# Another order of ScalarE's and VectorE's work in the first eleven steps of a fused recurrent mixer

## The chip, the cores and the metric

The kernel runs on one core of a Trainium2 chip. The metric is the device time of one execution in microseconds (us). TensorE is called PE in the profile (PEld is its weight load), VectorE is DVE, ScalarE is ACT, GpSimd is POOL and SyncE is SP.

## What is computed

```python
xn = layernorm(x)                                  # x: 4 x 256 x 512
zxbcdt = xn @ in_proj_w.T                          # gate 8192, x 8192, B and C 8*128 each, dt 128
xBC = silu(conv4(xBC) + conv_b)                    # causal, 4 taps, per channel
dt = softplus(dt + dt_bias); A = -exp(A_log)       # 128 heads of 64 channels, 8 groups
# per head: a linear recurrence; it is taken here in 2 chunks of 128 positions per sequence
Y[i] = sum over j <= i of (C_i . B_j) * exp(sum of A*dt over j+1..i) * x_j * dt_j
y = (Y + D*x) * silu(gate)
y = y * rsqrt(mean of y*y over a group of 1024 channels + eps) * norm_w
s = y @ out_proj_w.T
g = silu(ffn(xn))                                  # ternary weights, 512 -> 1792 -> 512
out = x + s * g
```

## The kernel before

All arithmetic is float32. A first part, `front`, makes the layer norm, the feed-forward network, dt, the scores C.B of the 8 groups and the running decay sums of the first 20 heads; in the profiled execution its last products on PE end at about 313.5 us. What follows is a loop over 64 channel tiles of 128 channels (two heads each), `for i in range(CT)`. Its order is written out by hand: under a manual schedule each engine works through its instructions in the order of the program, and waits are only for data and for buffers. The loop is a pipeline in which three tiles are under way at once. Step i

- projects tile i: x by way of `px` and `pq`, the gate by way of `pz` and others. It is a seven-product scheme of the Strassen kind. In the order of PE: **A** px = a11*x11, **B** pq = s1*t1, **C** px += s2*t2, **D** the first half of pz += a12*x21, **E** px += s3*t3, **F** the second half of pz, **G** px += a22*t4, **H** pq += s4*x22. A to H all have line 173. What stands in px is taken out by ACT after A (to pz, line 832), after C (to the gate's second half gT, line 842, "the gate's copy"), after E (to xpad, line 874) and after G (to xpad, line 902). Since C, E and G add to the same bank px, each has to wait for the copy before it;
- finishes tile i-1: convolution's SiLU (line 186), the exponentials of its two decay matrices m (line 627), "meet" (lines 630 and 631: m and the off-diagonal block mo are multiplied by the group's scores gm, on DVE), transposes of x on PE (tp, line 637, two ahead of E and two ahead of G, four behind H), values v on DVE (lines 645, 654), and 24 products for y (py, line 681);
- gates tile i-2 on DVE (line 688) and squares it on ACT (line 863); an accumulating DMA on POOL's queue (line 934) adds the squares to sqacc.

Steps 0 to 9 (`fill`) do no output projection yet. In these the sums of squares are made right behind the exponentials. In steps 1 to 10 (`lead`) both exponentials of tile i-1 stand in step i; from step 11 on the first of them is made at the end of the step before. Where ACT goes from SiLU to Exp or back, the trace shows an ACT_TABLE_LOAD of 1.28 us. On DVE the order behind "meet" is line 894 (xpad += pq, for which H waits, since it adds to pq), the values, the sums of the next weights (lines 142 to 146), the taps of the convolution (line 181) and line 915 (gT += pq). In steps 3 to 6 ACT scales two tiles of the output weights (line 882), in steps 7 and 8 DVE makes one sum of 1.22 us each for the output projection (lines 726, 727), and in step 10 the first sums of the output projection (lines 717 to 720), the sum of squares of group 0 (`norm_sums`, PE line 699, ACT line 702) and two scans (line 189) come in. Weights, rows of decays and scores come through SP's queue.

Of the kernel before, what the change touches and what calls it, by code (L numbers as in the profile page):

```python
# [51 lines left out]
NB = 4  # L52
L = 256
NC = 2
T = NB * L
# [21 lines left out]
HALF = T // 2  # L77
# [4 lines left out]
def mixer_ffn(ctx: ExitStack, tc: tile.TileContext, x, in_w, conv_w, conv_b, dt_bias, a_log, d_col,  # L82
              norm_w, out_w, gate_t, up_t, down_t, gate_s, up_s, down_s, out):
    nc = tc.nc
# [34 lines left out]
    gm = mc.tile([P, ROW], F32, name="gm")  # L119
# [16 lines left out]
    def blocks(w):  # L136
        return [w[:, n, k:k + 2, :] for n in (0, 1) for k in (0, 2)]

    def combine_to(s1, s2, s4, s3, w):

        a11, a12, a21, a22 = blocks(w)
        nc.vector.tensor_add(s1, a21, a22)
        nc.vector.tensor_sub(s2, s1, a11)
        yield
        nc.vector.tensor_sub(s4, a12, s2)
        nc.vector.tensor_sub(s3, a11, a21)
        yield

    def factors(w, s):
        a11, a12, a21, a22 = blocks(w)  # L150
        return a11, a12, a22, s[:, 0], s[:, 1], s[:, 2], a21
# [15 lines left out]
    def by_batch(v):  # L167
        return v.rearrange("p (b l) -> p b l", l=L)

    def product(pp, a, b, start, ks=range(KT // 2)):  # L170

        for k in ks:
            nc.tensor.matmul(pp, a[:, k, :], b[:, k, :], start=start and k == 0,  # L173
                             stop=k == KT // 2 - 1, skip_group_check=not start)

    def last_tap(i, xT, xpad):
        nc.scalar.mul(xT, xpad[:, :, TAPS - 1:], cw[:, i, TAPS - 1:TAPS])  # L177

    def conv_taps(i, xT, xpad, taps=range(TAPS - 1)):
        for k in taps:  # L180
            nc.vector.scalar_tensor_tensor(xT, xpad[:, :, k:k + L], cw[:, i, k:k + 1], xT,  # L181
                                           ALU.mult, ALU.add)

    def conv_silu(i, xT):
        xf = xT.rearrange("p b l -> p (b l)")
        nc.scalar.activation(xf, xf, AF.Silu, bias=cb[:, i:i + 1])  # L186

    def decay_scan(m):
        nc.vector.tensor_tensor_scan(m, m, after, 0.0, ALU.add, ALU.mult)  # L189
# [419 lines left out]
    def load_rows(ct):  # L609
        ms = []  # L610
        for h in range(2):
            m = mp.tile([P, T], F32, name="m")
            n = 2 * ct + h
            nc.sync.dma_start(m, early[n] if ct < EARLY else rows[n, 0:T].partition_broadcast(P))
            ms.append(m)
        return ms

    def load_off(ct):
        offs = []
        for h in range(2):  # L620
            m = mop.tile([P, NB * P], F32, name="mo")
            nc.sync.dma_start(m, rows[2 * ct + h, T:].partition_broadcast(P))
            offs.append(m)
        return offs

    def decay_exp(m):
        nc.scalar.activation(m, m, AF.Exp)  # L627

    def meet(m, off):
        nc.vector.tensor_mul(m, m, gm[:, 0:T])  # L630
        nc.vector.tensor_mul(off, off, gm[:, T:])

    def transposed(xT, c, bs=range(NB), tp=None):
        if tp is None:
            tp = ps_t.tile([P, NB, P], F32, name="tp", tag="t")
        for b in bs:
            nc.tensor.transpose(tp[:, b, :], xT[:, b, c * P:(c + 1) * P], ident)  # L637
        return tp
# [12 lines left out]
    def values_1(ct, xT):  # L651
        tp = transposed(xT, 1)
        v = xsp.tile([P, NB, 2, HD], F32, name="v")
        nc.vector.tensor_tensor(
            v, tp.rearrange("p b (h d) -> p b h d", d=HD),
            dt[:, 1, :, 2 * ct:2 * ct + 2].unsqueeze(3).to_broadcast([P, NB, 2, HD]), ALU.mult)
        return v

    def y_begin(ct, xT):

        ps = []
        for i in range(2):
            py = ps_y.tile([P, 2, L], F32, name="py", tag="y")
            nc.scalar.mul(py, xT[:, 2 * i:2 * i + 2, :], dcol[:, ct:ct + 1])
            ps.append(py)
        return ps
# [110 lines left out]
    with tc.manual_schedule():  # L777
        nc.sync.dma_start(gm, scores[0])
        ms, offs = {0: load_rows(0)}, {0: load_off(0)}
        xTs, gTs, yps, wos, rights, toms = {}, {}, {}, {}, {}, {}  # L780
        sqacc = sq = rs = ya = outs = left = nxt = ob = sa = sb = sc = None
        for i in range(CT):
            r, g = i % PER_G, i // PER_G
            here, old, older = True, i >= 1, i >= 2
# [8 lines left out]
            def project_out(between):  # L793
                nonlocal sa, sb, sc, outs
                if on % 2 == 0:
                    sa = osp.tile([P, NC, HID], F32, name="sa")
                    sb = osp.tile([P, NC, HH], F32, name="sb")
                    sc = osp.tile([P, HH], F32, name="sc", bufs=2)
                    outs = out_first(left, rights[og], leave)
                for n in range(4 - on % 2):  # L800
                    next(outs)
                    if n == 1:
                        between()
# [10 lines left out]
            fill = og < 0  # L814
# [11 lines left out]
            if here:  # L826
                a11, a12, a22, s1, s2, s4, s3 = a
                px, pq, pz = [ps_proj.tile([P, HALF], F32, name=f"p{n}", tag="proj")
                              for n in "xqz"]
                gT = gtp.tile([P, T], F32, name="gT")  # L830
                product(px, a11, x11, True)
                nc.scalar.copy(pz, px)
            lead = old and i - 1 < LEAD
            if lead:
                conv_silu(i - 1, xTs[i - 1])
                decay_exp(ms[i - 1][0])
            elif old:
                decay_exp(ms[i - 1][1])
            if here:
                product(pq, s1, t1, True)  # L840
                product(px, s2, t2, False)
                nc.scalar.copy(gT[:, HALF:], px)  # L842
                if lead:
                    decay_exp(ms[i - 1][1])
                if i >= EARLY:
                    decay_scan(ms[i][0])

                product(pz, a12, x21, False, (0,))
            if old:
                tp0 = transposed(xTs[i - 1], 0, (0, 1))  # L850
                meet(ms[i - 1][0], offs[i - 1][0])
                meet(ms[i - 1][1], offs[i - 1][1])
                if r == 0 and here:
                    nc.sync.dma_start(gm, scores[g])
                if not fill:
                    yps[i - 1] = y_begin(i - 1, xTs[i - 1])

            def square():
                nonlocal sq, sqacc
                yf = yg.rearrange("p b l -> p (b l)")  # L860
                first = (i - 2) % PER_G == 0
                sq = sqp.tile([P, T], F32, name="sqacc" if first else "sq")
                nc.scalar.activation(sq, yf, AF.Square)  # L863
                if first:
                    sqacc = sq

            if older and fill:
                square()
            if here:
                product(px, s3, t3, False)  # L870
                product(pz, a12, x21, False, (1,))
                if old:
                    transposed(xTs[i - 1], 0, (2, 3), tp0)
                nc.scalar.copy(xpad_h[1], by_batch(px))
            if old and fill:
                yps[i - 1] = y_begin(i - 1, xTs[i - 1])
# [27 lines left out]
            if fill:  # L904
                s = scp.tile([P, 3, KT // 2, P], F32, name="s")
                sums = combine_to(s[:, 0], s[:, 1], s[:, 2], blocks(w)[2], w)
                a = factors(w, s)
                next(sums)
                xTs[i] = xtp.tile([P, NB, L], F32, name="xT")
                last_tap(i, xTs[i], xpad)  # L910
                conv_taps(i, xTs[i], xpad, (0,))
                if old:
                    vs.append(values_1(i - 1, xTs[i - 1]))
            if here:
                nc.vector.tensor_add(gT[:, HALF:], gT[:, HALF:], pq)  # L915
                if og >= 0 and on == 0:
                    rs = small.tile([P, NT], F32, name="rs2", bufs=2)
                    nc.vector.reciprocal(rs, sd)
# [5 lines left out]
            if here:  # L924
                nc.scalar.activation(gT[:, 0:HALF], pz, AF.Silu)
                if og >= 0:
                    project_out(lambda: nc.scalar.activation(gT[:, HALF:], gT[:, HALF:], AF.Silu))
                else:
                    nc.scalar.activation(gT[:, HALF:], gT[:, HALF:], AF.Silu)
            if old:  # L930
                y_products(yps[i - 1], vs, ms.pop(i - 1), offs.pop(i - 1), fill)
            if older and (i - 2) % PER_G:
# [41 lines left out]
        last, ob = CT - 1, NB - 1  # L974
# [3 lines left out]
        decay_exp(ms[last][1])  # L978
        py = y_begin(last, xTs[last])
        vs = values_0(last, transposed(xTs[last], 0))  # L980
        for m, off in zip(ms[last], offs[last]):
            meet(m, off)
        sa = wp.tile([P, NC, KT, P], F32, name="w").rearrange("p n k m -> p n (k m)")
        sb = scp.tile([P, 3, KT // 2, P], F32, name="s")[:, 0:2].rearrange("p n k m -> p n (k m)")
        sc = osp.tile([P, HH], F32, name="sc", bufs=2)
# [14 lines left out]
        yg, gT = ygp.tile([P, NB, L], F32, name="yg"), gTs.pop(last)  # L1000
# [105 lines left out]
```

## Time and profile before

| | |
|---|---|
| median of three runs | 1743.87 us (1742.74 to 1744.98) |
| profiled execution, its own time | 1743.98 us |
| its span, from the first to the last instruction | 1742.3 us |
| granted clock of PE | 0.999 |
| PE busy, DVE busy, ACT busy | 1718.9, 1446.9, 1068.7 us |
| steps 0 to 10 | 313.5 to 500.1 us of the span |
| step 0, step 1 (from A to the next A) | 12.2, 18.7 us |
| steps 2 to 9 | 16.24, 16.32, 16.33, 16.32, 16.32, 16.58, 16.28, 16.24 us |
| step 10 | 25.0 us |

The profiled execution's time is 1.7 us above its span. In a timeline, each row has the start in us, the duration in us, the engine, the line, the operation, what it writes and reads, the number of instructions merged, and in brackets the idle time of the engine just before with what ended it. The matmuls' durations overlap, so the distance from one row's start to the next is what counts on PE.

### The profile page before, as it was taken

What the parts mean: (1) busy time and instruction counts of PE and PEld (TensorE: products, weight loads), DVE (VectorE), ACT (ScalarE), POOL (GpSimd) and SP (SyncE); (2) the same over time, 40 slices, a digit from 0 to 9 for tenths busy, and PEclk for the clock granted to TensorE, in tenths of its full rate; (3) what the DMA queues carried; (4) which work ended last, traced back from release to release, by engine and by line L of the source; (5) the groups of instructions that cost most, each with busy time, mean ns of one, the idle gap of its engine ahead of it and who ended that gap; (6) DMA issues with size and microseconds to landing.
All of it is one profiled execution on the core that took longest, in us unless ns stands there. A gap on an engine that the chain in (4) does not pass through costs nothing.

```text
span 1742.3 us, 22580 instructions
## 1 busy us (share of the span) xinstructions
PE 1718.9 (99%) x8494; PEld 1108.2 (64%) x8494; DVE 1446.9 (83%) x1742; ACT 1068.7 (61%) x1418; POOL 211.7 (12%) x238
## 2 busy tenths in 40 slices
PE   9999999999999999999999999999999999999999
PEld 7566666555566666666666666666666666666687
DVE  5768878577898898889888988898888888888876
ACT  4544333588776666666666666666666676667740
POOL 3312323000000000111011101110111011101110
PEclk9999999999999999999999999999999999999999
DMA  6266565567746676777677667776766677757785
GB/s 226 71 205 225 211 206 207 174 209 228 215 161 206 200 214 190 208 203 214 190 208 202 202 189 217 200 200 185 210 200 198 182 211 200 215 163 212 212 234 167
DMA packets 161931, 347.27 MB, mean 199 GB/s; under 512 B 15136, under 2 KB 52896, under 8 KB 161824
## 3 DMA queue, kind: packets, MB, share of 16 engines
q1 hardware_dynamic: 139136, 292.89, 48.8%
q0 software_dynamic: 22688, 52.96, 17.1%
q8 instruction: 67, 1.10, 0.2%
q14 instruction: 40, 0.33, 0.1%
HBM read 236.48 MB, written 81.00 MB: 182 GB/s over the span
## 4 chain that ended last, share of the span: by engine, by line
PE 89%; DVE 3%; ACT 3%; DMA 3%; issue 1%; SPq 1%; POOL 0%; ACTq 0%; DVEq 0%
PE px L173 26%; PE po L737 22%; PE pq L173 13%; PE py L681 10%; PE pz L173 7%; PE tp L637 3%; PE pp L288 3%; DMA w<-in_in_w 2%; PE pf L296 2%; PE pg L463 1%; PE pv L699 1%; DVE bT L181 1%; ACT m L627 1%; ACT xT L186 1%; DVE cT L181 0%
## 5 line engine op out<-in xcount | busy, mean ns | idle before, releaser
L173 PE MATMUL px<-xc,w 128*128 128x512 f32 x576 | 273.2, 597 | 8.4 <-ACT xpad L427 5.7
L181 DVE SCALAR_TENSOR_TENSOR xT<-xpad,cw,xT 128x1024 f32<-128x1024 f32 x192 | 246.1, 1282 | 14.2 <-ACT xT L177 10.0
L189 DVE TENSOR_TENSOR_SCAN m<-m,after 128x1024 f32<-128x1024 f32 x108 | 246.5, 2282 | 0.0
L737 PE MATMUL po<-wo,ya 128*128 128x256 f32 x768 | 176.5, 379 | 0.0
L630 DVE TENSOR_TENSOR m<-m,gm 128x1024 f32<-128x1024 f32 x128 | 155.0, 1211 | 21.1 <-ACT m L627 21.0
L681 PE MATMUL py<-m,v 128*64 128x128 f32 x2048 | 160.3, 276 | 0.0
L934 POOL DMA_DIRECT2D sqacc<-sq x54 | 46.1, 854 | 884.2 <-ACT sq L863 811.8
L173 PEld LDWEIGHTS px<-xc,w 128*128 128x128 f32 x576 | 98.9, 190 | 84.1 <-issue 68.9
L737 PEld LDWEIGHTS po<-wo,ya 128*128 128x128 f32 x768 | 141.5, 190 | 17.0 <-issue 0.2
L173 PE MATMUL pz<-xnT,w 128*128 128x512 f32 x288 | 145.8, 592 | 0.0
L173 PE MATMUL px<-xnT,w 128*128 128x512 f32 x288 | 141.8, 615 | 0.0
L173 PE MATMUL px<-xc,s 128*128 128x512 f32 x288 | 135.8, 594 | 2.3 <-ACT cpad L427 1.8
L173 PE MATMUL pq<-xnT,s 128*128 128x512 f32 x288 | 136.2, 595 | 0.1
L173 PE MATMUL pq<-xc,s 128*128 128x512 f32 x288 | 135.4, 592 | 0.7 <-DVE gT L915 0.7
L627 ACT ACTIVATE m<-m 128x1024 f32<-128x1024 f32 x128 | 135.4, 1058 | 0.7
L637 PEld LDWEIGHTS tp<-ident,xT 128*128 128x128 f32 x512 | 67.7, 140 | 100.0 <-issue 87.3
L681 PEld LDWEIGHTS py<-m,v 128*64 128x64 f32 x2048 | 117.1, 137 | 20.2 <-issue 19.1
L737 PE MATMUL po<-tw,sy 128*128 128x256 f32 x512 | 115.9, 379 | 0.0
L737 PEld LDWEIGHTS po<-tw,sy 128*128 128x128 f32 x512 | 97.2, 190 | 13.2
L842 ACT COPY gT<-px 128x512 f32<-128x512 f32 x64 | 37.3, 583 | 103.0 <-PE px L173 103.0
L681 PE MATMUL py<-mo,v 128*64 128x128 f32 x1024 | 99.4, 273 | 0.0
L173 PEld LDWEIGHTS pq<-xc,s 128*128 128x128 f32 x288 | 54.6, 190 | 69.9 <-issue 61.2
(178 smaller groups left out, 3118.3 us busy)
## 6 DMA issues: line engine op xcount, KB each, us to landing
m<-rows SPq DMA_DIRECT2D x108, 512.0 KB, 6.5
w<-in_in_w SPq DMA_DIRECT2D x144, 256.0 KB, 6.9
mo<-rows SPq DMA_DIRECT2D x128, 256.0 KB, 7.2
gated<-yg SPq DMA_DIRECT2D x64, 512.0 KB, 8.2
ya<-gated SPq DMA_DIRECT2D x30, 1024.0 KB, 7.1
sqacc<-sq POOLq DMA_DIRECT2D x54, 512.0 KB, 5.9
wo<-in_out_w SPq DMA_DIRECT2D x64, 256.0 KB, 7.0
acc<-sa POOLq DMA_DIRECT2D x23, 512.0 KB, 5.9
```

The lines of the kernel that those rows point to most:

```text
L173: nc.tensor.matmul(pp, a[:, k, :], b[:, k, :], start=start and k == 0, stop=k == KT // 2 - 1, skip_group_check=not start)
L181: nc.vector.scalar_tensor_tensor(xT, xpad[:, :, k:k + L], cw[:, i, k:k + 1], xT, ALU.mult, ALU.add)
L189: nc.vector.tensor_tensor_scan(m, m, after, 0.0, ALU.add, ALU.mult)
L288: nc.tensor.matmul(pp, w[:, k * P:(k + 1) * P], part[:, k, :], start=(k == 0 and part is xh), stop=(k == KT - 1 and part is xl))
L296: nc.tensor.matmul(pf, part[:, i * P:(i + 1) * P], wd, start=(f == 0 and part is hh), stop=(f == FT - 1 and part is hl))
L627: nc.scalar.activation(m, m, AF.Exp)
L630: nc.vector.tensor_mul(m, m, gm[:, 0:T])
L637: nc.tensor.transpose(tp[:, b, :], xT[:, b, c * P:(c + 1) * P], ident)
L681: nc.tensor.matmul(py[d, q * P:(q + 1) * P], v[:, b, h, :], m, start=False, stop=True, skip_group_check=True)
L737: nc.tensor.matmul(po, a[:, k, :], b[:, k, :], start=start and k == 0, stop=k == HG - 1, skip_group_check=not start)
L842: nc.scalar.copy(gT[:, HALF:], px)
L934: nc.gpsimd.dma_start(sqacc, sq, accum_op=ALU.add)
```

## The change

In steps 1 to 10 the gate's copy (line 842) stands ahead of both exponentials in ACT's order instead of between them. In step 1 the SiLU of tile 0 also goes behind the gate's copy, and its four transposes of the first chunk all go behind F. "Meet" multiplies both off-diagonal blocks first and both m after that, in every step. In steps 2 to 9 the square goes from behind the exponentials to the end of the step, behind the gate's SiLU. In step 0, line 915 goes ahead of the first tap on DVE. Nothing is added or left out.

```diff
-    def meet(m, off):
-        nc.vector.tensor_mul(m, m, gm[:, 0:T])
-        nc.vector.tensor_mul(off, off, gm[:, T:])
+    def meet(ms, offs):
+        for off in offs:
+            nc.vector.tensor_mul(off, off, gm[:, T:])
+        for m in ms:
+            nc.vector.tensor_mul(m, m, gm[:, 0:T])
...
             lead = old and i - 1 < LEAD
-            if lead:
+            if lead and i > 1:
                 conv_silu(i - 1, xTs[i - 1])
-                decay_exp(ms[i - 1][0])
-            elif old:
+            elif old and not lead:
                 decay_exp(ms[i - 1][1])
             if here:
                 product(pq, s1, t1, True)
                 product(px, s2, t2, False)
                 nc.scalar.copy(gT[:, HALF:], px)
+                if i == 1:
+                    conv_silu(0, xTs[0])
                 if lead:
+                    decay_exp(ms[i - 1][0])
                     decay_exp(ms[i - 1][1])
                 if i >= EARLY:
                     decay_scan(ms[i][0])
 
                 product(pz, a12, x21, False, (0,))
             if old:
-                tp0 = transposed(xTs[i - 1], 0, (0, 1))
-                meet(ms[i - 1][0], offs[i - 1][0])
-                meet(ms[i - 1][1], offs[i - 1][1])
+                tp0 = transposed(xTs[i - 1], 0, (0, 1) if i > 1 else ())
+                meet(ms[i - 1], offs[i - 1])
...
-            if older and fill:
-                square()
             if here:
                 product(px, s3, t3, False)
                 product(pz, a12, x21, False, (1,))
                 if old:
-                    transposed(xTs[i - 1], 0, (2, 3), tp0)
+                    transposed(xTs[i - 1], 0, (2, 3) if i > 1 else range(NB), tp0)
                 nc.scalar.copy(xpad_h[1], by_batch(px))
...
                 last_tap(i, xTs[i], xpad)
+                if i == 0:
+                    nc.vector.tensor_add(gT[:, HALF:], gT[:, HALF:], pq)
                 conv_taps(i, xTs[i], xpad, (0,))
...
             if here:
-                nc.vector.tensor_add(gT[:, HALF:], gT[:, HALF:], pq)
+                if i:
+                    nc.vector.tensor_add(gT[:, HALF:], gT[:, HALF:], pq)
...
                     nc.scalar.activation(gT[:, HALF:], gT[:, HALF:], AF.Silu)
+            if older and fill:
+                square()
             if old:
                 y_products(yps[i - 1], vs, ms.pop(i - 1), offs.pop(i - 1), fill)
...
-        for m, off in zip(ms[last], offs[last]):
-            meet(m, off)
+        meet(ms[last], offs[last])
```

## The prediction

> **What bounds the kernel.** I read the shares of engines and the chain that ended last first, both on the page.
>
> ```profile
> PE 1718.9 (99%) x8494; PEld 1108.2 (64%) x8494; DVE 1446.9 (83%) x1742; ACT 1068.7 (61%) x1418; POOL 211.7 (12%) x238
> ...
> PE 89%; DVE 3%; ACT 3%; DMA 3%; issue 1%; SPq 1%; POOL 0%; ACTq 0%; DVEq 0%
> ```
>
> PE is busy for 99% of the span and holds 89% of the chain. So an edit on ACT or DVE counts only by the time that PE waits, and nothing later gives a delay back. Next I read PE's timeline in step 2.
>
> ```profile
> 349.71 1.02 PE L173 MATMUL pz<-xnT,w 128*128 128x512 f32 x2
> 350.57 0.38 PE L637 MATMUL tp<-ident,xT 128*128 128x128 f32 x2
> 351.06 1.98 PE L173 MATMUL px<-xc,w 128*128 128x512 f32 x4
> 352.89 1.02 PE L173 MATMUL pz<-xnT,w 128*128 128x512 f32 x2
> 353.74 0.38 PE L637 MATMUL tp<-ident,xT 128*128 128x128 f32 x2
> 353.96 1.88 PE L173 MATMUL px<-xc,w 128*128 128x512 f32 x4
> 355.68 1.88 PE L173 MATMUL pq<-xnT,s 128*128 128x512 f32 x4
> ```
>
> These are D, two transposes, E, F, two transposes, G, H. From start to start the second pair of transposes takes 0.22 us, the first 0.49: E waits 0.27. G takes 1.72, E 1.83: a product after a wait costs 0.11 more (as B and E of step 1 do). So 0.38 us a step can be had at E, no more. ACT's timeline shows why, and what stands next to it.
>
> ```profile
> 347.02 1.15 ACT L186 ACTIVATE xT<-xT,cb 128x1024 f32<-128x1024 f32 x1
> 348.19 1.28 ACT L627 ACT_TABLE_LOAD   x1
> 349.48 1.06 ACT L627 ACTIVATE m<-m 128x1024 f32<-128x1024 f32 x1
> 350.44 0.57 ACT L842 COPY gT<-px 128x512 f32<-128x512 f32 x1
> 350.91 1.06 ACT L627 ACTIVATE m<-m 128x1024 f32<-128x1024 f32 x1
> 351.87 1.05 ACT L863 ACTIVATE sqacc<-yg 128x1024 f32<-128x1024 f32 x1
> 353.09 0.59 ACT L874 COPY xpad<-px 128x512 f32<-128x512 f32 x1 [0.17 <-PE px L173]
> ```
>
> The gate's copy ends at 351.01, and E starts 0.05 later. But the table load and the first exponential run while PE still makes C; they end about when C does. The copy for G ends at 353.68, 0.28 before G.
>
> **The change, part by part: steps 2 to 9.** I keep step 2's clock. C gives way to D at 349.71. A copy can start 0.20 after that (the xpad copy at 353.09 starts 0.20 after F took E's place), so the gate's copy runs from 349.91 to 350.50. E can start at 350.79: the 0.38 goes. Now the question is where the table load stands. The trace shows it in front of the activation that needs it and behind a copy that itself waits:
>
> ```profile
> 94.59 0.59 ACT L366 COPY dt<-tp 128x512 f32<-128x512 f32 x1 [5.12 <-PE tp L365]
> 95.19 1.28 ACT L558 ACT_TABLE_LOAD   x1
> 96.49 0.69 ACT L558 ACTIVATE sg<-pp,gs 128x512 f32<-128x512 f32 x1
> ```
>
> There ACT stood idle for 5.12 us and the load still came after the copy, 0.60 after its start, and the function 1.30 after that. So after the change the load no longer runs beside C: 349.91 copy, 350.50 load, 351.80 first exponential, 0.96 to the second (350.91 to 351.87 is such a distance) at 352.76, 0.96 to the xpad copy at 353.72, 0.59 for it, 0.05 to PE: G at 354.36. PE would be ready at 350.79 + 1.72 + 0.85 + 0.22 = 353.58. So G waits 0.78 and pays 0.11 for it. Net per step: -0.38 + 0.78 + 0.11 = **+0.51**. The square's 0.95, gone from this place, is already in that chain; without it the loss would be 1.46. Eight steps: +4.1.
>
> [...]
>
> What hides the rest. The square at the step's end: ACT's next copy waits for A (1.95 us idle before 362.77, the copy behind A), and the square needs 0.95 of it. Nothing stands behind the square on ACT but that copy; without this cover it would delay C by up to 0.95. DVE: both mo (0.60 each) move into DVE's wait of 2.26 us before m, so only two m follow: first m at 352.89, second 1.14 later at 354.03, line 894 at 355.17 to 355.86. It was at 354.05, so it is 1.1 late, but H starts at 354.36 + 1.83 = 356.19; 0.33 is left. The taps wait for ACT, as before, 2.0 us behind H.
>
> Where that cover is thinner:
> - Steps 3 to 6 (line 882): the copy behind G started 0.35 after H (step 3: 372.27 against 371.92), now 353.72 + 0.48 + 1.24 + 1.22 = 356.66, 0.47 after H. The values for the last y products were already just in time, so +0.11 each, **+0.4**.
> - Step 7: DVE's sum of line 726 (1.14) stands ahead of line 894. Line 894 ended at 437.39 and H started at 437.45; now the second m starts 4.32 after D, as in step 2, at 435.56, line 726 at 436.70, line 894 runs from 437.83 to 438.51, H at 438.56: +1.11, that is **+0.6** above the 0.51.
> - Step 8: line 727 stands ahead of the weights' sums and the taps. Line 894 comes 5.46 after D, at 453.29, the taps 0.60 + 0.60 + 0.60 + 1.13 + 0.46 + 0.34 behind it at 457.02; that is 2.7 after H (454.31) instead of 2.1, and the values for the last y products come 0.6 late: **+0.6**.
> - Step 10: ACT makes copy, load, exponentials, two products for y (1.23) and the xpad copy: G at 486.2, as before (486.30). But DVE: first m at 483.52 (was 481.20), second 484.66, four sums of 0.67 (lines 717 to 720), line 894 from 488.46 to 489.14; H at 489.2 instead of 488.10: **+1.1**.
>
> **Steps 0 and 1.** On PE B of step 1 waits 0.69 for line 915, and E 1.76 for the gate's copy:
>
> ```profile
> 328.28 1.98 PE L173 MATMUL pq<-xc,s 128*128 128x512 f32 x4 [0.69 <-DVE gT L915]
> ...
> 334.82 1.98 PE L173 MATMUL px<-xc,w 128*128 128x512 f32 x4 [1.76 <-ACT gT L842]
> ```
>
> Line 915 needs H of step 0, done when A starts at 325.72; 0.2 later it runs, until 326.60. Then B follows A at 327.44, C 329.16, D 330.88, E 331.74 (the gate's copy at 331.08 to 331.65). The tap now waits 0.17 longer, but no longer has line 915 behind it: the taps end at 330.22, before the copy. Then ACT: SiLU 331.55, load 332.72, exponentials 334.01 and 334.97, xpad copy 335.93 to 336.52, G 336.57 (was 337.72). PE would be ready at 334.84, so it waits here. A of step 2 moves from 344.46 to 343.4: **-1.0**.
>
> **Steps 11 to 63 and the tail.** Only the order of "meet" changes there. The list of waits has DVE waiting for an exponential 9 times, all of them in steps 1 to 9; later m and mo are both there, and the four together take the same time. SP: the reload of gm at step 8 waits for the last product with gm, 1.1 later within the step; it took 6.6 us to land and its reader is some 9 us off. I take nothing, with 1.1 us either way as bounds, the spread of the runs of before about their median.
>
> The accumulating DMA: in step 9 the square ends at 476.17 instead of 467.30, so the DMA goes out at 476.55. Its landing took 5.6 us in the middle, 10.8 at most, so 482.2 to 487.4. `norm_sums` would read at 484.2, and as H waits for DVE it can be 1.5 late for nothing. Taken at nothing (the middle); the upper end is +1.6.
>
> **The sum**, on the profiled execution: 4.1 + 0.4 + 0.6 + 0.6 + 1.1 - 1.0 = +5.8. Its own time 1743.98 is 0.1 above the median of the runs, so I add to it: **1749.8**.
>
> **Rivals.**
> 1. Faster: the load stands in the idle time between the SiLU and the gate's copy (348.19 to 349.91 is 1.72, it needs 1.30). It decides as soon as it does: the exponentials then start at 350.39, the xpad copy waits for E only, G is not held. -0.38 x 8, -0.3 in step 10 (line 894 then ends at 487.73 instead of 488.02), -1.0: -4.3, **1739.6**. For: the gap is there in each step. Against: the row at 94.59, and before SiLU at 357.67 it comes after five copies too. Chance 0.11.
> 2. Small loss: the lateness of DVE in steps 7, 8, 10 and of ACT in 3 to 6 is taken up by slack that I don't see. 4.1 - 1.0: **1747.1**. Chance 0.13, somewhat more than half of it within 0.2%.
> 3. The DMA of squares comes late at step 10 (10.8 us, as in step 9 of this trace): +1.6, **1751.4**. Chance 0.08.
> 4. The order on the engines comes out as before: **1744.0**. Chance 0.02.
>
> The forecast has 0.66. The range of 1745.5 to 1752.5 holds it with cases 2 and 3 and leaves out 1 and 4. A measurement of this kernel can't tell less than 0.2% (3.5 us) from no change: faster 0.11 (case 1), same 0.09 (0.07 of case 2, and case 4), slower 0.80.
>
> **What would show it.** Right: in steps 2 to 9 a row of the load behind the gate's copy, E with no wait, and PE idle or late at G behind "ACT xpad L874", with steps 2 and 9 of about 16.75 us, 3 to 6 of 16.9, 7 of 17.7, 8 of 17.4 and 10 of 26.1; A of step 2 about 1.0 earlier. Wrong: the load in front of the copy, or steps of 15.9; G in time though the load is behind the copy; or a difference behind step 11.

## The result and the profile after

The changed kernel takes 1750.28 us (median of 6 runs, 1747.70 to 1751.65) against 1743.64 us (6 runs, 1742.74 to 1744.98): a ratio of 1.0036, 95% interval 1.0025 to 1.0048. It is slower by 6.6 us in the medians, and by 6.05 us between the two profiled executions; 1749.8 was forecast. The profiled execution took 1750.03 us, its span 1748.3. From `meet` on, the lines of the file move by one to six: 842 is now 843, 874 is 875, 630 is 633, 894 is 895, 934 is 940.

The page, engines and chain that ended last:

```profile
PE 1719.1 (98%) x8494; PEld 1107.4 (63%) x8494; DVE 1447.2 (83%) x1742; ACT 1068.7 (61%) x1418; POOL 213.1 (12%) x238
...
PE 89%; DVE 4%; ACT 3%; DMA 2%; issue 1%; SPq 0%; POOL 0%; ACTq 0%; DVEq 0%
```

Each engine's busy time is the same to within 1.4 us; the span grew by 6.0. So the new time is waiting. PE's timeline in step 2 (D, two transposes, E, F, two transposes, G, H):

```profile
349.11 1.02 PE L173 MATMUL pz<-xnT,w 128*128 128x512 f32 x2
349.97 0.38 PE L639 MATMUL tp<-ident,xT 128*128 128x128 f32 x2
350.18 1.88 PE L173 MATMUL px<-xc,w 128*128 128x512 f32 x4
351.90 1.02 PE L173 MATMUL pz<-xnT,w 128*128 128x512 f32 x2
352.76 0.38 PE L639 MATMUL tp<-ident,xT 128*128 128x128 f32 x2
353.74 1.98 PE L173 MATMUL px<-xc,w 128*128 128x512 f32 x4 [0.59 <-ACT xpad L875]
355.56 1.88 PE L173 MATMUL pq<-xnT,s 128*128 128x512 f32 x4
```

E follows its transposes by 0.21: its wait is gone. G follows its own by 0.98, and the bracket names the xpad copy. ACT's timeline beside it:

```profile
346.41 1.15 ACT L186 ACTIVATE xT<-xT,cb 128x1024 f32<-128x1024 f32 x1
349.31 0.59 ACT L843 COPY gT<-px 128x512 f32<-128x512 f32 x1 [1.74 <-PE px L173]
349.91 1.28 ACT L627 ACT_TABLE_LOAD   x1
351.21 2.00 ACT L627 ACTIVATE m<-m 128x1024 f32<-128x1024 f32 x2
353.12 0.57 ACT L875 COPY xpad<-px 128x512 f32<-128x512 f32 x1
```

ACT stands idle for 1.74 us between the SiLU and the gate's copy, the table load comes only after that copy, and the xpad copy starts without any idle time, straight behind the exponentials. That is the chain that holds G.

The distance from one step's A to the next gives the account by steps (us, each from PE's timeline of the profiled execution):

| step | 0 | 1 | 2 | 3 | 4 | 5 | 6 | 7 | 8 | 9 | 10 |
|---|---|---|---|---|---|---|---|---|---|---|---|
| before | 12.23 | 18.74 | 16.24 | 16.32 | 16.33 | 16.32 | 16.32 | 16.58 | 16.28 | 16.24 | 25.02 |
| after | 12.23 | 17.66 | 16.72 | 16.94 | 16.93 | 16.95 | 16.94 | 17.71 | 17.39 | 16.72 | 26.15 |
| difference | 0 | -1.08 | +0.48 | +0.62 | +0.60 | +0.63 | +0.62 | +1.13 | +1.11 | +0.48 | +1.13 |

Together +5.7. Steps 11 to 62 differ by no more than 0.01 each, and what follows by 0.1 in all. The first A comes at 313.96 instead of 313.49; the change touches nothing ahead of it (see the last section).

### The profile page after: what moved, and what is told of

Read it like the earlier page. It is cut to its first block, busy times and chain, and to the rows that moved or that the text cites. A ratio compares the mean times of both kernels' runs of the same rounds, so it can differ in the third digit from the quotient of the medians.

```text
span 1748.3 us, 22563 instructions
## 1 busy us (share of the span) xinstructions
PE 1719.1 (98%) x8494; PEld 1107.4 (63%) x8494; DVE 1447.2 (83%) x1742; ACT 1068.7 (61%) x1418; POOL 213.1 (12%) x238
## 4 chain that ended last, share of the span: by engine, by line
PE 89%; DVE 4%; ACT 3%; DMA 2%; issue 1%; SPq 0%; POOL 0%; ACTq 0%; DVEq 0%
PE px L173 26%; PE po L739 22%; PE pq L173 14%; PE py L683 10%; PE pz L173 6%; PE pp L288 3%; PE tp L639 3%; DMA w<-in_in_w 2%; PE pf L296 2%; PE pg L463 1%; ACT m L627 1%; DVE bT L181 1%; ACT L627 1%; PE pv L701 1%; DVE cT L181 0%
## 5 line engine op out<-in xcount | busy, mean ns | idle before, releaser
L633 DVE TENSOR_TENSOR m<-m,gm 128x1024 f32<-128x1024 f32 x128 | 150.6, 1218 | 31.1 <-ACT m L627 31.1
```

## The experiments

The theory: the table load, now behind the gate's copy, makes ACT's chain from C to G longer than PE's work between them; DVE's lateness in H follows from it. The rivals: the moved square, meet's new order, or the copy's place as such costs the time. Where a ratio is given, it is to the kernel before, with its 95% interval. The columns 1 to 10 are the lengths of the steps in us, from one profiled execution each.

| kernel | 1 | 2 | 3 to 6 | 7 | 8 | 9 | 10 | ratio |
|---|---|---|---|---|---|---|---|---|
| copy_between | 17.66 | 16.24 | 16.32 | 16.25 | 16.24 | 16.24 | 25.77 | 0.9995 (0.9987 to 1.0004) |
| load_early | 17.66 | 15.87 | 15.94 | 16.30 | 15.99 | 15.87 | 27.93 | 0.9996 (0.9987 to 1.0005) |
| square_back | 17.67 | 17.66 | 17.89 | 17.71 | 17.67 | 17.66 | 26.14 | 1.0071 (1.0057 to 1.0084) |
| meet_back | 18.73 | 17.78 | 17.78 | 20.61 | 18.60 | 17.78 | 29.43 | 1.0109 (1.0093 to 1.0124) |
| copy_alone | 18.29 | 17.78 | 17.89 | 18.91 | 18.61 | 17.78 | 29.03 | 1.0098 (1.0082 to 1.0113) |
| after_again | 17.66 | 16.72 | 16.94 | 17.71 | 17.40 | 16.72 | 27.21 | 1.0034 (1.0022 to 1.0047) |
| before_again | 18.39 | 16.24 | 16.32 | 16.59 | 16.28 | 16.24 | 25.01 | one run |
| best | 17.66 | 15.87 | 15.94 | 16.30 | 15.99 | 15.94 | 29.21 | 0.9992 (0.9984 to 1.0001) |
| best_rows | 17.67 | 15.86 | 15.95 | 16.30 | 15.99 | 15.95 | 24.90 | 0.9982 (0.9973 to 0.9991) |

**copy_between**: the copy goes back, the rest of the change stays.

```diff
+                if lead and i > 1:
+                    decay_exp(ms[i - 1][0])
                 nc.scalar.copy(gT[:, HALF:], px)
                 if i == 1:
                     conv_silu(0, xTs[0])
+                    decay_exp(ms[0][0])
                 if lead:
-                    decay_exp(ms[i - 1][0])
                     decay_exp(ms[i - 1][1])
```

> The changed kernel, but with the gate's copy between the two exponentials again in steps 1 to 10; squares, meet and step 0 stay changed. If the table load behind the copy is the cause, the load and the first exponential run beside C again: steps 2 and 9 take 16.24 us, 3 to 6 16.3, step 7 some 16.3 (meet's new order leaves DVE earlier), step 8 16.3, step 10 25.0, step 1 17.7; 1.5 us faster than the kernel before, about 1742.2. If instead the squares at the step's end or meet's new order cost the time, the steps stay at 16.7 to 17.7 us and the time at 1750.

Steps 1 to 9 came out as the theory has them, to 0.06 us: the whole loss of steps 2 to 9 goes with the copy's place, and step 7 is 0.33 shorter than before, since meet's order has line 894 earlier. Step 10 was 0.8 longer than expected: there PE waited 0.58 us for the accumulating DMA of the squares. With it the kernel can't be told from the kernel before.

**load_early**: the changed kernel with one exponential of a 128x1 column more (`ahead_exp`, read by nobody).

```diff
             if lead and i > 1:
                 conv_silu(i - 1, xTs[i - 1])
+                nc.scalar.activation(ahead_exp, one, AF.Exp)
```

> The changed kernel with one exponential of a 128x1 column more, whose result nobody reads, between the SiLU and the gate's copy in steps 2 to 10: it draws the table load into ACT's 1.74 us of idle time there. If the load behind the copy is the cause, E and G both run without a wait: steps 2 and 9 take 15.86 us, 3 to 6 15.95, step 7 16.3, step 8 15.95, step 10 24.75; 4.3 us faster than the kernel before, about 1739.3. If the load costs nothing there and the two exponentials behind the copy are the cause by themselves, or if the switch of tables has a cost that idle time does not hide, the steps stay above 16.24 and the time at 1744 or more.

ACT's timeline in its step 2:

```profile
347.25 1.28 ACT L839 ACT_TABLE_LOAD   x1
348.55 0.20 ACT L839 ACTIVATE ahead_exp<-one 128x1 f32<-128x1 f32 x1
348.98 0.59 ACT L845 COPY gT<-px 128x512 f32<-128x512 f32 x1 [0.23 <-PE px L174]
349.46 2.00 ACT L628 ACTIVATE m<-m 128x1024 f32<-128x1024 f32 x2
351.77 0.59 ACT L877 COPY xpad<-px 128x512 f32<-128x512 f32 x1 [0.31 <-PE px L174]
```

The same copy, exponentials and xpad copy in the same order, but the load lies in what was idle time. The first exponential now starts 0.48 us after the copy instead of 1.90, and the xpad copy waits for PE again (the bracket), not PE for it. Steps 2 to 9 fell to 15.87 to 16.30, as expected. This settles the cause: the place of the load, not that of the copy. But step 10 took 27.93 instead of 24.75, and the gain of steps 1 to 9 (3.9 us) was mostly gone. PE's timeline there:

```profile
482.02 1.95 PE L702 MATMUL pv<-one,sqacc 128*128 128x1 f32 x16 [1.42 <-DMA sqacc<-sq]
483.83 3.58 PE L174 MATMUL px<-xc,w 128*128 128x512 f32 x4
487.20 2.01 PE L174 MATMUL pq<-xnT,s 128*128 128x512 f32 x4
```

The sum of squares waits for the DMA of a square that now ends with step 9, and the product behind it takes 3.37 us from start to start instead of 1.8.

**square_back**: the call of `square()` goes back behind the exponentials.

```diff
+            if older and fill:
+                square()
             if here:
                 product(px, s3, t3, False)
...
-            if older and fill:
-                square()
             if old:
                 y_products(...)
```

> The changed kernel with the square behind the exponentials again. If G waits for ACT's chain, the square's 0.95 us lengthens that chain: steps 2 and 9 17.67 us, 3 to 6 17.9, step 7 17.75 (there DVE was late anyway), step 8 17.7, step 10 unchanged at 26.15; 6 us slower than the changed kernel, about 1756. If the square at the end of the step is what costs the time, this is faster than the changed kernel, down to 1744.

As the theory has it, to 0.05 us in each step. ACT's timeline in step 2 shows the square in the chain:

```profile
351.73 2.00 ACT L627 ACTIVATE m<-m 128x1024 f32<-128x1024 f32 x2
353.64 1.04 ACT L866 ACTIVATE sqacc<-yg 128x1024 f32<-128x1024 f32 x1
354.59 0.57 ACT L877 COPY xpad<-px 128x512 f32<-128x512 f32 x1
```

The xpad copy starts 0.95 later than without it, and step 2 is 0.94 longer. So the square's move did not cost the time in steps 2 to 9; with the copy in its new place it saved some 0.95 us in each of steps 2 to 6 and 9, 0.28 in step 8 and nothing in step 7, where H waits for DVE.

**meet_back**: the old order of "meet", the rest of the change stays.

```diff
-        for off in offs:
-            nc.vector.tensor_mul(off, off, gm[:, T:])
-        for m in ms:
-            nc.vector.tensor_mul(m, m, gm[:, 0:T])
+        for m, off in zip(ms, offs):
+            nc.vector.tensor_mul(m, m, gm[:, 0:T])
+            nc.vector.tensor_mul(off, off, gm[:, T:])
```

> The changed kernel with meet in the old order (m, mo, m, mo). If DVE has only 0.33 us left ahead of H, two products of 0.60 behind the exponentials make line 895 end 1.2 later and H wait: steps 2 to 6 and 9 17.74 us, step 1 18.6, step 7 18.9, step 8 18.5, step 10 27.3; 9.7 us slower than the changed kernel, about 1760. If meet's order is of no account, or costs time itself, the time stays at 1750 or falls.

DVE in step 2, then PE:

```profile
354.47 1.22 DVE L631 TENSOR_TENSOR m<-m,gm 128x1024 f32<-128x1024 f32 x1 [4.85 <-ACT m L627]
355.61 0.68 DVE L632 TENSOR_TENSOR mo<-mo,gm 128x512 f32<-128x512 f32 x1
356.21 1.22 DVE L631 TENSOR_TENSOR m<-m,gm 128x1024 f32<-128x1024 f32 x1
357.35 0.69 DVE L632 TENSOR_TENSOR mo<-mo,gm 128x512 f32<-128x512 f32 x1
357.95 0.68 DVE L894 TENSOR_TENSOR xpad<-xpad,pq 128x512 f32<-128x512 f32 x1
```

```profile
358.68 1.98 PE L173 MATMUL pq<-xnT,s 128*128 128x512 f32 x4 [0.79 <-DVE xpad L894]
```

Both mo stand behind the exponentials, and H waits 0.79 us for line 894: step 2 is 1.06 us longer than in the changed kernel, so meet's new order saves time and does not cost it. The steps other than 7 and 10 came within 0.13 us of what was expected. Steps 7 and 10 were 1.7 and 2.1 us longer than expected: in step 7 H took 3.48 us from start to start, at a granted clock of 0.50, instead of 1.72, and in step 10 G took 3.56 instead of 1.80 (last section).

**copy_alone**: the kernel before with only the copy moved.

```diff
             if lead:
                 conv_silu(i - 1, xTs[i - 1])
-                decay_exp(ms[i - 1][0])
...
                 if lead:
+                    decay_exp(ms[i - 1][0])
                     decay_exp(ms[i - 1][1])
```

> The kernel before with one edit: the gate's copy ahead of both exponentials in steps 1 to 10. Squares, meet, step 0 and the transposes of step 1 stay as before. If the load behind the copy lengthens ACT's chain to G and the two other edits only soften that, the chain has the square in it too and DVE has both mo behind the exponentials: steps 2 and 9 17.7 us, 3 to 6 17.9, step 7 18.9 or more, step 8 18.5, step 10 27.3 or more; about 16 us slower than the kernel before, a ratio of 1.009. If the copy's new place is a gain that the other two edits spoil, the steps take 15.9 us and the time is 3 us below that of the kernel before.

It lost 17.3 us. So the copy's new place is no gain that the other edits spoil; with them 6.6 of the 17.3 us are left. Some of the 17.3 is a slower PE: in step 10 H waited 2.21 us for DVE and then took 3.03 us from start to start, against 1.82 behind the wait of 0.99 in the changed kernel.

**after_again** and **before_again** are both kernels a second time.

> The changed kernel a second time, to see what varies between its executions. If the steps' lengths are set by waits of the engines on each other, steps 1 to 9 repeat within 0.05 us, 17.66, 16.72, 16.94 four times, 17.71, 17.39, 16.72; step 10 may differ by the landing of the accumulating DMA (26.1, or up to 1.6 more); the first A of the loop moves by up to 1.7 us with a stretch of half clock near 298 us.

> The kernel before a second time. Steps 1 to 10 repeat within 0.05 us: 18.74, 16.24, 16.32 four times, 16.58, 16.28, 16.24, 25.02. If the half clock near 298 us, which the changed kernel's profile shows and that of before does not, has nothing to do with the change, it can show here too, and then the first A comes up to 1.7 us after 313.5.

Steps 2 to 9 repeat to 0.01 us. What varies is outside them. Step 10 of the changed kernel took 27.21: PE waited 0.68 us for the squares' DMA, and then G took 2.72 and H 2.49 us from start to start, against 1.80 and 1.71 in copy_between, where PE waited 0.58 us for the same DMA. Step 1 of the kernel before took 18.39 instead of 18.74, so the expectation of 0.05 failed there: in the first profile, line 177 of step 0 on ACT waited 0.38 us for a DMA of `ffn`, in this one not, and line 915 and B came that much earlier. The first A came at 312.32, 1.17 earlier than in the first profile, with a mean granted clock of 1.00 in both profiles in each of seven stretches of at most 50 us up to 312; so a lower clock is not all that moves it.

**best** and **best_rows** are load_early with edits that try to keep what it gains. best makes the square of step 9 alone behind the products for y; best_rows also sends the first row of decays ahead of the load of ya in SP's queue in step 9.

```diff
             if old and fill:
                 yps[i - 1] = y_begin(i - 1, xTs[i - 1])
+            if i == PER_G + 1:
+                square()
...
-            if older and fill:
+            if older and fill and i != PER_G + 1:
                 square()
```

> load_early with the square of step 9 alone moved forward, behind the two products for y, where ACT has some 1.0 us idle. In load_early PE waited 1.4 us at step 10 for the accumulating DMA of that square and then made G at half the clock. If the late square is the cause, its DMA now goes out some 5 us earlier in the step, PE's wait is gone and G takes 1.7 us again: step 10 takes 24.75 us instead of 27.93, steps 2 to 9 stay at 15.87 to 16.3, and the time falls 3.2 us below load_early's and 4.4 us below that of the kernel before (a ratio of 0.9975). If the DMA was late by itself, whenever it goes out, step 10 stays at 27 to 28 us.

The squares were in time, yet step 10 took 29.21. The timeline of DVE and PE in step 10:

```profile
478.38 2.29 DVE L190 TENSOR_TENSOR_SCAN m<-m,after 128x1024 f32<-128x1024 f32 x1 [2.53 <-DMA m<-rows]
...
487.43 3.01 PE L174 MATMUL pq<-xnT,s 128*128 128x512 f32 x4 [2.69 <-DVE xpad L899]
```

DVE waits for the row of decays, H for DVE. On SP's queue that row's transfer stood behind the load of ya, which went out only at 467.65, 7.7 us after the store of the last gated tile it reads. So best_rows puts the row first:

```diff
-                if r == 1 and i >= PER_G and here:
+                if r == 1 and i > PER_G + 1 and here:
                     nxt = load_gated((i - PER_G) // PER_G, 0)
...
                 if i + 1 < CT:
-                    ms[i + 1] = load_rows(i + 1)
+                    ms[i + 1] = load_rows(i + 1, load_first if i == PER_G + 1 else None)
```

(`load_first` loads ya of group 0, and `load_rows` calls it behind its first transfer.)

> best with one edit more, in step 9: the load of ya (1 MB of gated tiles, which waits for the last gated tile to land) goes out behind the first row of decays for step 10 instead of ahead of it. In best DVE's scan of step 10 waited 2.53 us for that row, H of step 10 then 2.69 us for DVE, and PE fell to half the clock. If the row was late because it stood behind ya in SP's queue, it now goes out some 7 us earlier, the scan does not wait, and step 10 takes 24.75 us instead of 29.2; steps 1 to 9 stay at 17.66, 15.87, 15.94 four times, 16.3, 16.0, 15.9; 4.3 us below the kernel before, a ratio of 0.9975. If the transfers as a whole are too many for a shorter step 9, something else is late instead (ya for line 720, or the row) and step 10 stays above 26.

G and H of step 10 on PE:

```profile
482.62 1.96 PE L174 MATMUL px<-xc,w 128*128 128x512 f32 x4
484.66 1.98 PE L174 MATMUL pq<-xnT,s 128*128 128x512 f32 x4
```

H follows G by 2.04, and no scan waits. The kernel takes 1740.83 us against 1743.98 (12 and 17 runs): a ratio of 0.9982 (0.9973 to 0.9991), 3.1 us faster than the kernel before, where 4.3 was expected. In its profile steps 1 to 10 are 3.9 us shorter, and the first A comes 0.51 later, at 314.00. It is the only one of these whose interval lies below 1.

## Why the prediction was right

- **The load stands behind the copy.** Read from one row at 94.59 of the trace of before, and so it came: 349.91 behind the copy of 349.31. load_early shows that this place is the cause.
- **The chain from D to G** was put at 4.65 us and measured 4.63 (349.11 to 353.74). The step's loss was put at 0.51 and is 0.48; the 0.03 lie in the last copy, 0.57 instead of 0.59, and in roundings.
- **Steps 3 to 6** (0.62 forecast, 0.60 to 0.63), **7** (1.11, 1.13), **8** (1.1, 1.11) and **10** (1.1, 1.13) came from following line 894 and line 181 on DVE, and line 882 on ACT. In step 10 PE's timeline, then DVE's, show the forecast wait of H:

```profile
491.31 1.96 PE L173 MATMUL px<-xc,w 128*128 128x512 f32 x4
494.26 1.98 PE L173 MATMUL pq<-xnT,s 128*128 128x512 f32 x4 [0.99 <-DVE xpad L895]
```

```profile
488.59 2.36 DVE L633 TENSOR_TENSOR m<-m,gm 128x1024 f32<-128x1024 f32 x2 [1.21 <-ACT m L627]
...
493.53 0.68 DVE L895 TENSOR_TENSOR xpad<-xpad,pq 128x512 f32<-128x512 f32 x1
```

- **Steps 0 and 1**: -1.0 forecast (its own times, 344.46 and 343.4, give -1.06), -1.08 measured. B and E run on without a wait, and G is what waits now, as worked out:

```profile
334.85 0.60 PE L639 MATMUL tp<-ident,xT 128*128 128x128 f32 x4
337.01 1.98 PE L173 MATMUL px<-xc,w 128*128 128x512 f32 x4 [1.56 <-ACT xpad L875]
```

- **The squares' DMA** (taken at nothing, up to +1.6): in the first profile it landed 7.9 us after its issue instead of the 5.6 taken, just at the reading; the term was 2.3 short, and that it cost nothing was partly luck. In the second the wait was 0.68 us, and step 10 was 1.06 longer. The prediction had up to 1.5 of such lateness free, since H waits for DVE; but behind that wait G took 2.72 instead of 1.80 from start to start, and for that the sum had no term. That rival is a part of the spread of the runs, and it was the first limit that the faster kernels met.
- **The load's cost** was taken from the row at 94.59, 0.60 from the copy to the load and 1.30 from the load to the function, and so it came: 1.90 from copy to exponential (349.31 to 351.21). In load_early, without the load between them, the same distance is 0.48, so the load in this place cost 1.42 in all.
- **Not foreseen**: the first A 0.47 later, which no step of the sum had, and which is as large as a step's loss. Added to 1743.98, steps 1 to 10 alone give 1749.70. Between two profiles of one kernel, step 10 differed by 1.06, step 1 by 0.35 and the first A by up to 1.17. So the mechanism and the steps 2 to 9 were right to hundredths; that the total agrees to better than about 1 us is luck.

## What to carry to other kernels

When an instruction of ACT is moved, look at which table loads move with it: in these traces a load stands in front of the first activation that needs it (at 95.19 behind a copy of 94.59, at 349.91 behind one of 349.31), so a copy put ahead of that activation also pushes the load of 1.28 us out of the idle time it had. In load_early a one-column activation of 0.20 us brought the load back into the 1.74 us in which ACT waited anyway. And when a step gets shorter, the next limit may stand in a queue: here first the squares' DMA (1.42 us of PE's time in load_early), then a row of decays behind a load that itself waited (2.53 us of DVE's in best).

## What the runs showed of the hardware

In meet_back PE waited 1.93 us ahead of H in step 7, and the granted clock fell to half behind that. The stretches of its profile (us, PE busy, granted clock, DMA share, GB/s):

```profile
447.00:448.00 1.00, 0.00 (x0) 1.00 0.11 45
448.00:449.00 1.00, 0.28 (x1) 0.92 0.00 0
449.00:450.00 1.00, 1.00 (x2) 0.50 0.00 0
450.00:451.00 1.00, 1.00 (x2) 0.50 0.00 0
451.00:452.00 1.00, 1.00 (x2) 0.50 0.00 0
452.00:453.00 1.00, 1.00 (x9) 0.87 0.00 0
```

H, which began at 448.72, took 3.48 us from start to start instead of 1.72: the wait of 1.93 cost 1.76 again. From the 0.92 and 0.87 at its two ends, the half clock lasted from an estimated 448.84 to 452.26.

Other waits of PE, with what the product behind them took, from PE's timelines. In the rows of before and after the granted clock stayed at 1.00:

| profile, step | PE's wait, us | product behind it | from start to start, us |
|---|---|---|---|
| best, 10 | 2.69 | H | 2.80 |
| copy_alone, 10 | 2.21 | H | 3.03 |
| before, 1 | 1.76 | E | 1.83 |
| after, 1 | 1.56 | G | 1.83 |
| copy_alone, 9 | 1.53 | G | 1.84 |
| load_early, 10 | 1.42, ahead of `norm_sums` | G | 3.37 |
| meet_back, 10 | 1.25, ahead of `norm_sums` | G | 3.56 |
| after_again, 10 | 0.68, ahead of `norm_sums` | G | 2.72 |
| copy_between, 10 | 0.58, ahead of `norm_sums` | G | 1.80 |

The length of the wait alone does not order these rows: the product took 2.72 us behind a wait of 0.68 and 1.83 behind one of 1.76. What decides it was not shown.

A lower clock also bears on the first A's place. In `front` PE waits some 3 us for line 186: 3.12 in the first profile of before, 3.02 in the first of the changed kernel. In the changed kernel a granted clock of 0.50 followed, from 297.88 to 301.28, and the mean from 295 to 312 was 0.90; in both profiles of before that mean was 1.00. The wait of the changed kernel ended 1.08 earlier (296.80 against 297.88), and yet its first A came 0.47 later. The nine profiles of other kernels have the first A between 313.6 and 315.1, the two of before at 312.3 and 313.5, and `front` is the same code in all of them. Against an effect of the change speaks that of the 54 runs of before beside the experiments 27 have a granted clock of 0.997 or 0.998, below the 0.999 and 1.000 of its two profiles, so stretches of a lower clock occur in that kernel too; where they lie is not on record. That the 0.47 is no effect of the change is therefore likely, but not shown.
